# Pairing output blocks of two experts in a graph and mixture-of-experts kernel

## The chip, the cores and the metric

The kernel runs on one core of one Trainium2 chip. A core has TensorE (matmuls), VectorE, ScalarE, GpSimd and SyncE (SP), each with its own queue of instructions, and DMA engines that move data between HBM and the core. The metric is the device time of one execution in microseconds. Of the kernel before there are three runs: 798.14, 800.93 and 804.83 us, median 800.93 us.

## What is computed

The reference is one layer of a graph network, followed by a mixture of experts, on 625 nodes of 512 numbers. In short:

```python
x = x + relu(h_self + agg)          # h_self = LN(x) @ W_self.T + b_self
# agg: for each of 5000 edges, H_all[rel, tail] is added at its head
#      and H_all[rel + 8, head] at its tail; H_all = 16 relations of LN(x)
h = LN(x)                           # (625, 512)
router_logits = h @ router_w.T      # 16 experts
top_vals, top_idx = jax.lax.top_k(router_logits, 2)
weights = softmax(top_vals)         # two experts for each token
for wg, wu, wd, ce in experts:      # ce: the expert's weight for a token, or 0
    hid = silu(h @ wg) * (h @ wu)   # 512 -> 1024
    y = hid @ wd                    # 1024 -> 512
    acc = acc + ce[:, None] * y
out = x + acc
```

All is in float32. An expert's three matrices are 2 MB each. The kernel computes an expert only for the tokens that chose it.

## The kernel before

**First part.** For each of the 16 relations TensorE makes a table of transformed rows (L226), which goes to HBM as h_tab. GpSimd gathers the rows of the edges, 128 at a time (L466), in the order of a list made at L455. A one-hot matmul adds each gathered set into its tile of 128 nodes (L501, L508, L509). There are five tiles, 0 to 4, the last with fewer nodes. The messages of a tile come in stages; `add(j, s)` takes those of stage `s` for tile `j`, and `early_of` and `late` at L455 are the lists of the last two stages. When a tile has all its messages, its generator `rest(j)` does the routing: logits, the two best experts, and the place of each token among its expert's tokens (`place`). A hand-written list of steps sets how these generators and the messages alternate.

**Units.** The tokens of an expert are cut into units of 32. For one unit GpSimd fetches the tokens' rows (L682 for the first units, `fetch` at L848 for the others, up to eight units ahead), VectorE turns them (`turned`, L702), TensorE computes gate and up (`gate_up`, L714: 16 matmuls, four tiles of 32 columns at each of four steps of k), and ScalarE and VectorE make silu(gate) * up and turn it into hidT (`gated`, L726 to L732). A float32 matmul appears as two records in the trace. The PSUM tiles `o` of units are four.

**Output blocks.** `down` multiplies the hidden values of one expert's units with the expert's down matrix wd, over 8 steps of k. With more than two units it does one matmul per k of n * 32 columns on all 512 outputs (L745). With two units it does two matmuls per k, each of 64 columns on 256 outputs, which lie in the two halves of the partitions (L751). ScalarE copies the block out of PSUM (L757, or L759 with a weight), and GpSimd adds it into out in HBM by token (L760). Each such scatter waits for the one before it.

**Which experts and in what order.** Experts 0 to 2 (`NS = 3`) have three units each (`SU = 3`) before the ranking of the experts by load is known; the first two units of each (`SA = 2`) are told before tile 4 is routed, by `told_first` and `get_first`. These nine units are named o00 to o22, by expert and unit. Then come 13 ranks, in this order:

```python
RANKS = (3, 6, 3, 1)
ORDER = [12, 9, 10, 0, 11, 3, 4, 5, 6, 7, 8, 1, 2]
```

Ranks 0 to 2 have two units, 3 to 8 three, 9 to 11 four, and rank 12 (`r5`) five, as a block of three and one of two. The output block of one group of units is issued behind the units of the next (`waiting`, L1093 on). The words rank and expert are both used for these below.

**Tables.** `table` (L1026) multiplies one-hot matrices with what is to be told to each unit: `_t` (tokens, into `pw`), `_0` (weights of the first nine units, into `pv0`), and `_w` (weights of all other units, into `pw_w`). Their right sides val_t, val and val_w are made by VectorE at L1019. In the order on TensorE `_0` and a part of `_w` stand before the last five of the nine units, the rest of `_w` after them.

**Weights.** `load_expert` (L166) issues three loads on SP, gate, up and down (L176), into one of three pools that are used in turn. A load waits until the last matmul that reads the old contents of its buffer is done, and what stands behind it on SP waits too. The order of instructions on an engine is that of the program, except where the scheduler moves them by its own estimates; `tc.issue_after` holds some of them behind a named instruction.

## Time and profile before

| what | from | value |
|---|---|---|
| median of three runs | times | 800.93 us |
| the profiled execution | times | 802.45 us |
| its span, first to last instruction | page | 800.5 us |
| TensorE busy | page | 728.1 us, 91% |
| VectorE busy | page | 421.2 us, 53% |
| ScalarE busy | page | 133.1 us, 17% |
| GpSimd busy | page | 260.2 us, 32% |
| mean granted TensorE clock | cores | 0.950 |
| first unit starts | timeline of TensorE | 499.12 us |
| nine first units end | timeline of TensorE | 541.05 us |
| last output block ends | timeline of TensorE | 789.9 us |

The page gives busy time and the idle time before groups of instructions, with what ended it. The timeline lists the work of an engine in order: start, length, engine, line, operation, and in brackets the idle time before it and what it waited for. The busy time by window gives, for each stretch, the engines' busy time and counts, the granted clock as a share of full speed, the busy share of the DMA engines and what they moved. Ends of matmuls are modelled, so a busy TensorE need not be at its peak; starts are measured.

### The profile page before, as it was taken

The numbers are of one execution on the slowest core, as the hardware profiler recorded it, in microseconds if no ns is written. First come the engines' busy times: TensorE is split into PE (matmuls) and PEld (weight loads), VectorE is DVE, ScalarE is ACT, GpSimd is POOL, SyncE is SP. The second block draws the span as 40 slices with busy tenths as digits, with TensorE's granted clock in tenths as the row PEclk, the third lists the DMA queues.
The fourth block names the chain that finished last, engine by engine and source line by source line (L and its number), as shares of the span: only waits on it lengthen the run. The fifth ranks groups of instructions, "written<-read, shape, count | busy, mean of one in ns | idle before, by whom it ended". The sixth has DMA issues, their size and how long they took to land. (4 is left out here: it accounts for less than half of the span.)

```text
span 800.5 us, 9617 instructions
## 1 busy us (share of the span) xinstructions
PE 728.1 (91%) x3305; PEld 323.1 (40%) x3305; DVE 421.2 (53%) x1096; ACT 133.1 (17%) x252; POOL 260.2 (32%) x253
## 2 busy tenths in 40 slices
PE   5999998899968999959969986899999999999994
PEld 2444443355534555424535544223333333333332
DVE  7299937689758997426745837633223122222110
ACT  2000002223113332213322302000101001110010
POOL 1000017660275640575375352206333132200011
PEclk9999998999997999988988977889999999999998
DMA  6376449674487872786676397828999899999951
GB/s 205 127 261 236 178 139 298 210 246 151 140 266 231 261 234 74 234 280 188 217 221 188 126 365 287 296 87 301 387 382 366 312 390 395 383 394 389 381 189 15
DMA packets 77063, 200.70 MB, mean 251 GB/s; under 512 B 7636, under 2 KB 8072, under 8 KB 77008
## 3 DMA queue, kind: packets, MB, share of 16 engines
q1 hardware_dynamic: 46400, 125.57, 42.5%
q0 software_dynamic: 17936, 52.03, 22.7%
q10 hardware_dynamic: 12672, 22.42, 7.4%
q8 instruction: 28, 0.46, 0.2%
q14 instruction: 27, 0.22, 0.1%
HBM read 173.83 MB, written 26.87 MB: 251 GB/s over the span
## 5 line engine op out<-in xcount | busy, mean ns | idle before, releaser
L226 PE MATMUL o<-wt,xT 128*128 128x512 f32 x680 | 317.5, 611 | 2.7 <-ACT xT L217 2.7
L466 POOL DMA_INDIRECT g<-h_tab,rows x176 | 182.8, 1039 | 286.8 <-issue 151.3
L226 PEld LDWEIGHTS o<-wt,xT 128*128 128x128 f32 x680 | 131.7, 197 | 138.6 <-issue 130.6
L714 PE MATMUL o<-wgu,xbT 128*32 128x512 f32 x1600 | 179.0, 604 | 1.3 <-DVE in_unit L642 1.3
L505 ACT CAST hi<-g 128x512 fp32r<-128x512 f32 x158 | 91.3, 617 | 253.9 <-PE m L508 98.1
L507 DVE TENSOR_TENSOR lo<-g,hi 128x512 fp32r<-128x512 f32 x158 | 104.6, 688 | 40.5 <-ACT hi L505 23.8
L702 DVE STREAM_TRANSPOSE xbT<-xb 128x128 f32<-128x128 f32 x50 | 15.4, 310 | 165.8 <-PE o L714 156.6
L714 PEld LDWEIGHTS o<-wgu,xbT 128*32 128x32 f32 x1600 | 51.5, 112 | 123.9 <-issue 122.6
L508 PE MATMUL m<-hi,to 128*128 128x512 f32 x158 | 81.5, 516 | 20.4 <-issue 10.1
L745 PE MATMUL y<-wd,hidT 128*96 128x512 f32 (+1 forms) x208 | 91.9, 596 | 0.0
L295 DVE TENSOR_TENSOR hs<-o,bt 128x512 f32<-128x512 f32 x80 | 54.9, 688 | 60.6 <-PE o L226 33.4
L509 PE MATMUL m<-lo,to 128*128 128x512 f32 x158 | 70.5, 446 | 15.2 <-issue 6.8
L848 POOL DMA_INDIRECT xb<-hn_rows,get x41 | 39.2, 955 | 78.6 <-DVE xbT L702 49.7
L760 POOL DMA_INDIRECT out<-ys,adds x14 | 21.5, 1533 | 116.9 <-ACT ys L757 113.9
L745 PEld LDWEIGHTS y<-wd,hidT 128*96 128x96 f32 (+1 forms) x208 | 34.3, 169 | 56.7 <-issue 56.7
L508 PEld LDWEIGHTS m<-hi,to 128*128 128x128 f32 x158 | 30.6, 194 | 40.2 <-issue 21.7
L509 PEld LDWEIGHTS m<-lo,to 128*128 128x128 f32 x158 | 30.8, 195 | 38.5 <-issue 17.2
L726 ACT ACTIVATE sil<-o 128x256 f32<-128x256 f32 x50 | 19.2, 383 | 159.4 <-PE o L714 153.1
L416 DVE TENSOR_TENSOR val<-oc,vals 128x528 f16<-128x528 f16 x56 | 38.0, 709 | 0.0
L731 DVE SCALAR_TENSOR_TENSOR hid<-sil,weight,o 128x256 f32<-128x256 f32 x41 | 19.7, 481 | 30.1 <-ACT sil L726 26.4
L491 DVE TENSOR_TENSOR to<-count_f,node 128x512 fp32r<-128x512 f32 (+4 forms) x50 | 30.8, 623 | 6.1 <-issue 5.0
L401 DVE TENSOR_TENSOR at<-count_h,slot_p 128x768 f16<-128x768 f16 x28 | 26.7, 952 | 5.0 <-remote 5.0
(223 smaller groups left out, 354.2 us busy)
## 6 DMA issues: line engine op xcount, KB each, us to landing
wgu<-in_gate_w SPq DMA_DIRECT2D x16, 2048.0 KB
wgu<-in_up_w SPq DMA_DIRECT2D x16, 2048.0 KB
wd<-in_down_w SPq DMA_DIRECT2D x16, 2048.0 KB
h_tab<-hs ACTq DMA_DIRECT2D x80, 256.0 KB
wt<-in_w_rel SPq DMA_DIRECT2D x16, 1024.0 KB
bt<-in_b_rel SPq DMA_DIRECT2D x16, 256.0 KB
g<-h_tab,rows POOLq DMA_INDIRECT x176
xs<-in_x SPq DMA_DIRECT2D x5, 256.0 KB
```

What stands on the lines that cost most here:

```text
L226: nc.tensor.matmul(o, xT[:, k, ts(j, P)], wt[:, k, :], start=(k == 0), stop=(k == KD - 1))
L295: nc.vector.tensor_tensor(hs, linear(wt, j), bt, ALU.add)
L416: nc.vector.tensor_tensor(val[:, :, i, :], oc, vals[:, cs, i : i + 1].to_broadcast([P, SG, NCH]), ALU.mult)
L466: nc.gpsimd.indirect_dma_start(out=g, out_offset=None, in_=h_tab[d][: n * NP, :], in_offset=bass.IndirectOffsetOnAxis(ap=found[d][0][:, c ...
L491: nc.vector.tensor_tensor(to[:, :n], count_f[:, None, :].to_broadcast([P, n, P]), found[d][1][:, c : c + n, None].to_broadcast([P, n, P]), ...
L505: nc.scalar.copy(hi, g)
L507: nc.vector.tensor_tensor(lo, g, hi, ALU.subtract)
L508: nc.tensor.matmul(m, at, hi, start=first, stop=False)
L509: nc.tensor.matmul(m, at, lo, start=False, stop=last)
L714: last = nc.tensor.matmul(o[ts(c, Q), :].rearrange("p (s m i) -> p s m i", s=2, i=Q), xbT[:, k, :], wgu[:, k].rearrange("p s (m c i) -> p ...
L745: nc.tensor.matmul(y[: n * Q, :], hidT[:, k, :], wd[:, k, :], start=(k == 0), stop=(k == KF - 1))
L848: nc.gpsimd.indirect_dma_start(out=xb, out_offset=None, in_=hn_quarters, in_offset=bass.IndirectOffsetOnAxis(ap=get, axis=0),)
```

## The change

Four things change together.

1. `down` is divided. `add_outputs` takes pieces of one or two experts. Three units of one expert and one unit of another make one block of 128 rows: per k one matmul of 64 columns and two of 32, all on 512 outputs, of which the first two read one expert's wd and the third the other's. The two units that stay over from the second expert make a block in halves. The pairs are e0 with e1, e2 with the first unit of r5, and ranks 3 with 4, 5 with 6 and 7 with 8; the other four units of r5 make a block of their own. A block of two experts is added to out by two scatters, one after the other: the first takes the first 96 rows, the second all 128 with places that lie outside for rows not its own (`other_slots`, `AWAY`).
2. `load_expert` is divided into `load_hidden` (gate and up) and `load_output` (down). In the loop over ranks the gate and up of the next rank are issued before the down matrix of this one.
3. Softmax is issued earlier, and the tables of weights later: `_0` is held behind the eighth unit's last matmul and `_w` behind the ninth's. On TensorE both now follow the nine units, together with `_t`.
4. All of tile 3's last messages are gathered before the last two stages of tile 4, and the list of steps is changed to match.

```diff
--- before.py
+++ after.py
@@ -163,18 +163,32 @@
     n_again = const.tile([1, 1], I32, name="n_again")
     early = []
-    def load_expert(e):
+    def load_hidden(e):
         pool = wts[0]
         wts.append(wts.pop(0))
-        wgu = pool.tile([P, KD, 2, F], F32, name="wgu")
-        wd = pool.tile([P, KF, D], F32, name="wd")
-        for t, w in ((wgu[:, :, 0, :], gate_w), (wgu[:, :, 1, :], up_w), (wd, down_w)):
+        def load(t, w):
             s = w[e] if isinstance(e, int) else w[ds(e, 1)].rearrange("o k f -> (o k) f")
             behind = tc.issue_after(early.pop(0)) if early else nullcontext()
             with behind:
                 nc.sync.dma_start(t, s.rearrange("(k p) f -> p k f", p=P))
-        return wgu, wd
+        wgu = pool.tile([P, KD, 2, F], F32, name="wgu")
+        load(wgu[:, :, 0, :], gate_w)
+        load(wgu[:, :, 1, :], up_w)
+        def load_output():
+            wd = pool.tile([P, KF, D], F32, name="wd")
+            load(wd, down_w)
+            return wd
+        return wgu, load_output
+    def load_expert(e):
+        wgu, load_output = load_hidden(e)
+        return wgu, load_output()
     agg = act.tile([P, NT * D], F32, name="agg")
@@ -452,7 +466,7 @@
         early_of, late = ([cell[1, STAGES[1][g], j] for j in range(NT)] for g in (2, 3))
         relations_of = {(d, c): n for d, n, c0, cap, _ in plan for c in range(c0, c0 + cap)}
         order = [dc for _, cs in own_cells for dc in cs]
-        for cs in early_of[:4] + [late[0], late[1], early_of[4], late[2], late[3], late[4]]:
+        for cs in early_of[:4] + late[:4] + [early_of[4], late[4]]:
             order += cs
         order = [(d, relations_of[d, c], c) for d, c in order]
         assert len(set(order)) == 2 * NCH
@@ -735,33 +749,49 @@
             t = work.tile([P, KF, P], F32, name="hidT", bufs=3)
             return t if n == NQ else t.rearrange("p k t -> p (k t)")[:, : KF * n * Q].rearrange("p (k t) -> p k t", k=KF)
-        def down(wd, hidT, n, add, weight=None):
+        def down(y, pieces, wide):
+            for k in range(KF):
+                c = 0
+                for wd, hidT, g, n in pieces:
+                    if not wide:
+                        tiles = ((g, n, 0, slice(0, D // 2)), (g, n, 2, slice(D // 2, D)))
+                    elif n == 3:
+                        tiles = ((g, 2, c, slice(0, D)), (g + 2, 1, c + 2, slice(0, D)))
+                    else:
+                        tiles = ((g, n, c, slice(0, D)),)
+                    for u, m, at, cols in tiles:
+                        nc.tensor.matmul(
+                            y[at * Q : (at + m) * Q, : cols.stop - cols.start],
+                            hidT[:, k, u * Q : (u + m) * Q], wd[:, k, cols],
+                            start=(k == 0), stop=(k == KF - 1),
+                        )
+                    c += n
+        def add_outputs(pieces, add, weight=None):
+            wide = sum(n for *_, n in pieces) == 4
             y = py.tile([P, D], F32, name="y")
             ys = work.tile([P, D], F32, name="ys")
-            if n > 2:
-                for k in range(KF):
-                    nc.tensor.matmul(y[: n * Q, :], hidT[:, k, :], wd[:, k, :], start=(k == 0), stop=(k == KF - 1))
-                rows, width, to = n * Q, D, out
+            down(y, pieces, wide)
+            width, to = D, out
+            if not wide:
+                width, to = D // 2, out.rearrange("n (h d) -> (n h) d", h=2)
+            if weight is None:
+                nc.scalar.copy(ys[:, :width], y[:, :width])
             else:
-                for k in range(KF):
-                    for h in range(2):
-                        nc.tensor.matmul(
-                            y[ts(h, HP), : D // 2], hidT[:, k, :], wd[:, k, ts(h, D // 2)],
-                            start=(k == 0), stop=(k == KF - 1),
-                        )
-                rows, width, to = P, D // 2, out.rearrange("n (h d) -> (n h) d", h=2)
-            if weight is None:
-                nc.scalar.copy(ys[:rows, :width], y[:rows, :width])
-            else:
-                nc.scalar.mul(ys[:rows, :width], y[:rows, :width], weight[:rows])
-            nc.gpsimd.indirect_dma_start(
-                out=to, in_=ys[:rows, :width], in_offset=None,
-                out_offset=bass.IndirectOffsetOnAxis(ap=add[:rows], axis=0),
-                bounds_check=NP * D // width - 1, oob_is_err=False, compute_op=ALU.add,
-            )
+                nc.scalar.mul(ys[:, :width], y[:, :width], weight)
+            for i in range(len(pieces)):
+                rows = P if i == len(pieces) - 1 else pieces[0][3] * Q
+                nc.gpsimd.indirect_dma_start(
+                    out=to, in_=ys[:rows, :width], in_offset=None,
+                    out_offset=bass.IndirectOffsetOnAxis(ap=add[:rows, i : i + 1], axis=0),
+                    bounds_check=NP * D // width - 1, oob_is_err=False, compute_op=ALU.add,
+                )
         hn_quarters = hn_rows.rearrange("n (q d) -> (n q) d", q=NQ)
         xb0 = ract.tile([P, SU, NS, P], F32, name="xb0")
@@ -789,7 +819,7 @@
         early.extend(3 * stored)
         weights = [weights0, load_expert(1)]
-        for step in ((1, 3), 0, (4, 3), 0, (2, 3), 1, 0, 1, 0, 2, 1, (3, 3), 2, 1, 2, 3, 2, (4, 2), 3, 3, 3):
+        for step in ((1, 3), 0, 0, (2, 3), 1, 0, 1, 0, (3, 3), 2, 1, 2, 1, (4, 3), 3, 2, 3, 2, (4, 2), 3, 3):
             if isinstance(step, int):
                 next(tiles[step])
             else:
@@ -859,6 +889,11 @@
             nc.vector.tensor_tensor(row, row, token, ALU.add)
             nc.vector.tensor_scalar(row, row, -1.0, None, op0=ALU.add)
             return row
+        def other_slots(add, row):
+            nc.vector.tensor_scalar(add, row, 0.0, AWAY, op0=ALU.mult, op1=ALU.add)
+            nc.vector.tensor_copy(add[ts(NQ - 1, Q)], row[ts(NQ - 1, Q)])
         def by_slot(add, row, step, n):
@@ -993,14 +1028,13 @@
         last_units = []
         def last_unit():
-            for e in range(1, NS):
-                last_units.append(begun(e, 2))
-                last = steps(range(KD), last_units[-1])
-            last_units.append(last)
+            last_units.extend(begun(e, 2) for e in range(1, NS))
+            last_units.extend([steps(range(KD), o) for o in last_units])
         side, ends = units_of(place, cap, start, last_unit)
-        o12, o22, last = last_units
+        o12, o22, last_but, last = last_units
         gated(o21[0], None, hidT0[2], 1)
+        softmax()
         def of_units(unit, n, name):
             mine = mact.tile([P, 2 * NT, n], BF16, name=f"mine{name}")
@@ -1048,59 +1082,75 @@
         nc.vector.tensor_copy(who, pw)
         token, get_i = rows_to_get(who, "")
-        softmax()
         gated(o02[0], None, hidT0[0], 2)
         gated(o12[0], None, hidT0[1], 2)
         last_hid = gated(o22[0], None, hidT0[2], 2)
         pv0 = pr.tile([P, SU * NS, 3], F32, name="pv0", tag="pT")
-        table(mine0.rearrange("p c g s -> p c (g s)"), told[:, :, :, 2:], pv0, "_0")
+        with tc.issue_after(last_but):
+            table(mine0.rearrange("p c g s -> p c (g s)"), told[:, :, :, 2:], pv0, "_0")
         who0 = mact.tile([P, SU * NS, 3], F32, name="who0")
         nc.vector.tensor_copy(who0, pv0)
         nc.vector.tensor_scalar(token0, pw0, 1.0 / NQ, None, op0=ALU.mult)
         weight0 = summed(who0, "_0").rearrange("p (g s) -> p g s", s=NS)
         row0 = rows_to_add(token0.rearrange("p g s -> p (g s)"), "_0").rearrange("p (g s) -> p g s", s=NS)
-        add0 = mact.tile([P, NS], I32, name="add0")
+        halves0 = mact.tile([P, 2], F32, name="halves0")
+        nc.vector.tensor_scalar(halves0, row0[:, 1:, 1], 2.0, half, op0=ALU.mult, op1=ALU.add)
+        add0 = mact.tile([P, NS, 2], I32, name="add0")
         by0 = mact.tile([P, NS], F32, name="by0")
+        nc.vector.memset(by0, 1.0)
         for g in range(SU):
-            nc.vector.tensor_copy(add0[ts(g, Q), :], row0[ts(g, Q), g, :])
-            nc.vector.tensor_copy(by0[ts(g, Q), :], weight0[ts(g, Q), g, :])
+            nc.vector.tensor_copy(add0[ts(g, Q), ::2, 0], row0[ts(g, Q), g, ::2])
+            nc.vector.tensor_copy(by0[ts(g, Q), ::2], weight0[ts(g, Q), g, ::2])
+        other_slots(add0[:, 0, 1:], row0[:, 0, 1:2])
+        nc.vector.tensor_copy(by0[ts(3, Q), 0:1], weight0[ts(3, Q), 0, 1:2])
+        for q in range(NQ):
+            nc.vector.tensor_copy(add0[ts(q, Q), 1, 0:1], halves0[ts(q, Q), q % 2 : q % 2 + 1])
+            nc.vector.tensor_copy(by0[ts(q, Q), 1:2], weight0[ts(q, Q), 1 + q % 2, 1:2])
         pw_w = pr.tile([P, NU, 3], F32, name="pw_w", tag="pT")
-        table(mine, told[:, :, :, 2:], pw_w, "_w")
+        with tc.issue_after(last):
+            table(mine, told[:, :, :, 2:], pw_w, "_w")
         who_w = mact.tile([P, NU, 3], F32, name="who_w")
         nc.vector.tensor_copy(who_w, pw_w)
         weight = summed(who_w, "")
-        for e in range(NS):
-            down(weights[e][1], hidT0[e], SU, add0[:, e : e + 1], by0[:, e : e + 1])
+        wd0 = [w[1] for w in weights]
+        add_outputs([(wd0[0], hidT0[0], 0, 3), (wd0[1], hidT0[1], 0, 1)], add0[:, 0], by0[:, 0:1])
+        add_outputs([(wd0[1], hidT0[1], 1, 2)], add0[:, 1], by0[:, 1:2])
         to_row = rows_to_add(token, "")
...
-        blocks = []
-        for r in ORDER:
+        other_slots(add0[:, 2, 1:], to_row[:, C5 : C5 + 1])
+        adds4 = mact.tile([P, RANKS[2]], I32, name="adds4")
+        by_slot(adds4, to_row[:, C4:C3], 4, 4)
+        adds5 = mact.tile([P, 1], I32, name="adds5")
+        by_slot(adds5, to_row[:, C5 + 1 : C2], 4, 4)
+        adds3 = mact.tile([P, RANKS[1] // 2, 2], I32, name="adds3")
+        by_slot(adds3[:, :, 0], to_row[:, C3:C5], 6, 3)
+        other_slots(adds3[:, :, 1], to_row[:, C3:C5].rearrange("p (i s) -> p i s", s=6)[:, :, 3])
+        pairs3 = to_row[:, C3:C5].rearrange("p (i s) -> p i s", s=6)[:, :, 4:]
+        pairs2 = to_row[:, C2:].rearrange("p (i s) -> p i s", s=2)
+        halved = {}
+        for n, pairs in ((3, pairs3), (2, pairs2)):
+            nc.vector.tensor_scalar(pairs, pairs, 2.0, half, op0=ALU.mult, op1=ALU.add)
+            halved[n] = mact.tile([P, pairs.shape[1]], I32, name=f"halved{n}")
+            for q in range(NQ):
+                nc.vector.tensor_copy(halved[n][ts(q, Q), :], pairs[ts(q, Q), :, q % 2])
...
+        load_next()
+        waiting = []
+        for i, r in enumerate(ORDER):
+            if i > 0:
+                load_next()
+            wgu, load_output = loaded[i]
+            wd = load_output()
+            if i == 0:
+                load_next()
+            us = columns_of(r)
+            hid = [hidden(1), hidden(4)] if r == r5 else [hidden(len(us))]
+            for g, u in enumerate(us):
                 with tc.issue_after(last_hid):
                     xbT = turned(rows.pop(0))
                 o, _ = gate_up(wgu, xbT)
-                gated(o, weight[:, c + g : c + g + 1], hidT, g)
+                at_g = (hid[0], 0) if r == r5 and g == 0 else (hid[-1], g - (r == r5))
+                gated(o, weight[:, u : u + 1], *at_g)
                 fetch_next()
-            if waiting is not None:
-                down(*waiting)
-            i = (c - first[n]) // n
-            waiting = (wd, hidT, n, adds[n][:, i : i + 1])
-        down(*waiting)
+            for job in waiting:
+                add_outputs(*job)
+            waiting = []
+            if r == r5:
+                add_outputs([(wd0[2], hidT0[2], 0, 3), (wd, hid[0], 0, 1)], add0[:, 2], by0[:, 2:3])
+                waiting.append(([(wd, hid[1], 0, 4)], adds5))
+            elif r >= r4:
+                waiting.append(([(wd, hid[0], 0, 4)], adds4[:, r - r4 : r - r4 + 1]))
+            elif r >= r3:
+                k = (r - r3) // 2
+                if (r - r3) % 2 == 0:
+                    kept = wd, hid[0]
+                else:
+                    add_outputs([(*kept, 0, 3), (wd, hid[0], 0, 1)], adds3[:, k])
+                    add_outputs([(wd, hid[0], 1, 2)], halved[3][:, k : k + 1])
+            else:
+                waiting.append(([(wd, hid[0], 0, 2)], halved[2][:, r : r + 1]))
+        for job in waiting:
+            add_outputs(*job)
         n_more = mact.tile([1, 1], I32, name="n_more")
...
+                add_outputs([(wd, hidT, 0, NQ)], add)
```

More of the change, by code (lines that the diff above doesn't have):

```diff
@@ L1074 @@
         weight = summed(who_w, "")
-        for e in range(NS):
-            down(weights[e][1], hidT0[e], SU, add0[:, e : e + 1], by0[:, e : e + 1])
+        wd0 = [w[1] for w in weights]
+        add_outputs([(wd0[0], hidT0[0], 0, 3), (wd0[1], hidT0[1], 0, 1)], add0[:, 0], by0[:, 0:1])
+        add_outputs([(wd0[1], hidT0[1], 1, 2)], add0[:, 1], by0[:, 1:2])
         to_row = rows_to_add(token, "")
-        nc.vector.tensor_scalar(to_row[:, C5 + 3 :], to_row[:, C5 + 3 :], 2.0, half, op0=ALU.mult, op1=ALU.add)
@@ L1081 @@
-        adds = {}
-        for n, c, e in ((4, C4, C3), (3, C3, C5 + 3), (2, C5 + 3, NU)):
-            adds[n] = mact.tile([P, (e - c) // n], I32, name=f"adds{n}")
-            by_slot(adds[n], to_row[:, c:e], n, n)
-        for g in range(2):
-            nc.vector.tensor_copy(
-                adds[2][ts(2 + g, Q), :],
-                to_row[ts(2 + g, Q), C5 + 3 : NU].rearrange("p (i s) -> p i s", s=2)[:, :, g],
-            )
-        blocks = []
-        for r in ORDER:
-            if r == r5:
-                blocks += [(r, C5, 3), (r, C5 + 3, 2)]
-            elif r >= r4:
-                blocks.append((r, C4 + 4 * (r - r4), 4))
-            elif r >= r3:
-                blocks.append((r, C3 + 3 * (r - r3), 3))
-            else:
-                blocks.append((r, C2 + 2 * r, 2))
@@ L1102 @@
-        ahead = 8
-        columns = [u for _, c, n in blocks for u in range(c, c + n)]
+        other_slots(add0[:, 2, 1:], to_row[:, C5 : C5 + 1])
[6 more added lines that the diff above has]
+        other_slots(adds3[:, :, 1], to_row[:, C3:C5].rearrange("p (i s) -> p i s", s=6)[:, :, 3])
@@ L1104, with columns_of @@
+        def columns_of(r):
+            if r == r5:
+                return range(C5, C2)
+            if r >= r4:
+                return range(C4 + 4 * (r - r4), C4 + 4 * (r - r4) + 4)
+            if r >= r3:
+                return range(C3 + 3 * (r - r3), C3 + 3 * (r - r3) + 3)
+            return range(C2 + 2 * r, C2 + 2 * r + 2)
+        columns = [u for r in ORDER for u in columns_of(r)]
         rows = []
@@ L1109, in fetch_next, with load_next @@
                 rows.append(fetch(get_i[:, u : u + 1]))
-        for _ in range(ahead):
+        for _ in range(8):
             fetch_next()
-        first = {4: C4, 3: C3, 2: C5 + 3}
-        held = waiting = None
-        for r, c, n in blocks:
-            if r != held:
+        loaded = []
+        def load_next():
+            if len(loaded) < len(ORDER):
+                r = ORDER[len(loaded)]
                 e = nc.values_load(
@@ L1120 @@
                 )
-                wgu, wd = load_expert(e)
-                held = r
-            hidT = hidden(n)
-            for g in range(n):
+                loaded.append(load_hidden(e))
+        load_next()
[10 more added lines that the diff above has]
+            for g, u in enumerate(us):
                 with tc.issue_after(last_hid):
@@ L1242 @@
                     gated(o, weight[:, g : g + 1], hidT, g)
-                down(wd, hidT, NQ, add)
+                add_outputs([(wd, hidT, 0, NQ)], add)
 def kernel(x, src, dst, edge_type_8, L0_gnn_W_self, L0_gnn_b_self, L0_gnn_W_rel, L0_gnn_b_rel,
```

## The prediction

> **What bounds the kernel now.** I read the page's forty slices first (TensorE 9 tenths busy nearly everywhere after 640 us), then busy time by window from 498 us to the end.
>
> ```profile
> 498.00:505.00 7.00, 5.88 (x32) 1.48 (x36) 2.70 (x15) 0.68 (x1) 2.82 (x3) 0.52 0.99 332
> ...
> 514.00:522.00 8.00, 2.41 (x31) 0.73 (x24) 7.73 (x29) 0.38 (x1) 3.44 (x3) 0.77 0.40 131
> 522.00:526.00 4.00, 4.00 (x27) 1.33 (x30) 1.57 (x9) 0.00 (x0) 0.00 (x0) 0.61 0.02 6
> 526.00:534.00 8.00, 8.00 (x80) 2.44 (x76) 2.04 (x5) 0.77 (x2) 0.00 (x0) 1.00 0.00 0
> ...
> 640.00:700.00 60.00, 60.00 (x460) 19.99 (x452) 14.49 (x36) 6.22 (x16) 17.34 (x16) 1.00 1.04 389
> 700.00:760.00 60.00, 60.00 (x373) 19.26 (x366) 12.74 (x31) 5.58 (x13) 4.86 (x4) 1.00 1.03 388
> 760.00:771.00 11.00, 11.00 (x75) 3.33 (x74) 1.85 (x4) 1.35 (x3) 1.43 (x1) 1.00 0.96 334
> 771.00:790.00 19.00, 18.91 (x140) 8.06 (x138) 1.85 (x4) 1.72 (x4) 2.99 (x2) 1.00 0.14 22
> 790.00:800.50 10.50, 0.00 (x0) 0.00 (x0) 0.00 (x0) 0.37 (x1) 1.56 (x1) 0.73 0.14 19
> ```
>
> The columns are window and its length, busy time of TensorE, its weight loads, VectorE, ScalarE and GpSimd, then granted clock, DMA share and GB/s. From 522 us TensorE never rests until 789.9 us; the DMA is as full from 562 to 771 us, but its last 19 us are empty. So TensorE sets the end, with the weights 15 us behind it. The last 10.6 us are the copy and scatter of the last block. The timeline of TensorE gives the price of each block, and the place of the one hole:
>
> ```profile
> 499.12 11.51 PE L714 MATMUL o<-wgu,xbT 128*32 128x512 f32 x80 [1.26 <-DVE in_unit L642]
> ...
> 522.00 0.47 PE L1026 MATMUL pw_w<-val_w,at 128*128 128x123 bf16 x3 [5.59 <-DVE val_w L1019]
> 522.43 18.69 PE L714 MATMUL o<-wgu,xbT 128*32 128x512 f32 x160
> ```
> ```profile
> 579.87 7.11 PE L745 MATMUL y<-wd,hidT 128*96 128x512 f32 x16
> 586.91 13.94 PE L714 MATMUL o<-wgu,xbT 128*32 128x512 f32 x128
> 600.78 3.67 PE L751 MATMUL y<-wd,hidT 128*64 128x256 f32 x32
> 604.38 13.94 PE L714 MATMUL o<-wgu,xbT 128*32 128x512 f32 x128
> 618.25 7.13 PE L745 MATMUL y<-wd,hidT 128*128 128x512 f32 x16
> ...
> 782.78 7.13 PE L751 MATMUL y<-wd,hidT 128*64 128x256 f32 x64
> ```
>
> A unit (16 matmuls, two records each) is 13.94 / 4 = 3.48 us. An output block costs 7.05 us from start to start (579.87 to 586.91) whether it has 96 or 128 columns; a block in halves 3.60 (600.78 to 604.38). A three-unit block pays for a column group that it leaves empty.
>
> **The change, part by part.**
>
> Output blocks. Before, 13 full blocks (e0, e1, e2, three units of r5, three ranks of four units, six of three) and 4 in halves. After, 9 full (e0+e1, e2+r5, r5's other four, the three fours, three pairs of ranks) and 7 in halves (e1's two, two of each pair, ranks 0 to 2). If a mixed block costs what a full one does: 4 x 7.05 - 3 x 3.60 = 17.4 us less on TensorE. All of it is on the path, since TensorE has no hole there.
>
> Five of the nine are mixed: per step of k a tile of 64 columns, then two of 32. No row shows this. What the trace has is uniform: 32-column tiles start four at a time every 0.43 us, 64-column halves two every 0.215 us, a full tile one every 0.43 us. Columns times time is the same in all, which speaks for 0.86 us a step in the mixed block too. Against it stands the Trainium skill, "TensorEngine Tiling (Array Packing)", section Tiling Modes, under Key Properties: changing the mode, not just the tile, drains TensorE; its list has 128x64 and 128x32 as modes, none of both. The mixed block changes twice a step, 16 times a block, 80 times in all. The nearest rows are the changes at block edges: the last L714 record starts at 600.256 and the first L751 at 600.777, 0.52 us where the pitch is 0.43; back, 604.074 to 604.382, 0.31 where it is 0.215. So a change costs 0.09 to 0.10 us, up to 0.17 with the slower step after it. By the rows' columns alone the five blocks add nothing; by the rule at the row's price they add 80 x 0.1 = 8 us (0 to 13.6). I take 8: net 9.4 less. A gain from switching is excluded, since no group runs faster than its columns.
>
> Scatters go from 17 to 20, as each mixed block writes twice, one after the other. One takes about 1.5 us on GpSimd (row of L760: 21.5 us in 14) and the next can start 2.7 us later. They queue ahead of fetches of xb, which run eight units (28 us) ahead: two scatters, 8.6 us, hide there. If that cover went, each would cost TensorE up to 4.3 us. At the end two half blocks now follow each other at 3.6 us, less than 4.3: the tail grows by 0.7, to 11.3 us. ScalarE copies 128 rows for 96 (585 against 581 ns): nothing.
>
> Weights' loads. Gate and up of the next expert are issued before this one's down matrix on SP. In the timeline of SP a down load waits for its buffer until TensorE ends the block (wd at 744.36, then gate at 745.24), with everything behind it on SP. With gate and up ahead the pairs can hold both down matrices without stopping the stream. The DMA needs 17.7 us per expert (twelve between 548.9 and 770.9 with about 4 idle, including fetches and scatters); a pair takes TensorE 2 x 10.5 + 8.65 + 3.6 = 33.2 us against 35.4 of DMA, so there the weights are the pacer, and eat into the 15 us by which they lead. I count zero, and check the floor below.
>
> Early stage. Tile 3's three late gathers move ahead of tile 4's three first ones (1.256 us each on GpSimd, about 3.8 us), and its messages before tile 4's. The first fetch needs tiles 0 to 3, waits 20.6 us for its list and starts at 494.2; so o00 may start 3.8 us sooner, 495.3. The tables of weights, L1026, are told after the ninth unit instead of between units; the 5.59 us hole goes, and with it the slow steps behind it (granted clock 0.61 from 522 to 526: 1.6 us). What is late next: TensorE comes to o02 after o20 and o21 (7 us), at 512 + 7 = 519 us, where its xb was transposed at 519.99 in the trace; and o22 waits for the PSUM buffer that o20's hid frees, which stands behind val_w (1.40 us) on VectorE. These overlap in part: I charge 1.5 us (0 if VectorE is early, 4 if it keeps its times and both add up with the told tables). The steps at half clock at the start stay. Saved: 3.8 + 5.6 + 1.6 - 1.5 = 9.5; for e2's weights (issued 496.4, gate and up landing no sooner than 507) I round down to 8 (4 to 9). Fourteen more small copies on VectorE, about 0.16 to 0.22 us each, lie beside output blocks where it is 5.5 of 7.9 us busy: nothing; without that cover 2.8 us.
>
> Floor by DMA: r5's gate and up come with e0's last unit, its down with the first block, both 8 to 9 us sooner. The stream that ended at 770.9 ends near 762; after it only the last half block is needed, 3.6 us: 766. TensorE ends at 789.9 - 9.4 - 8 = 772.5, later, so it still decides.
>
> Sum: 772.5 + 11.3 = 783.8 us of span, against 800.5. The profiled execution was 802.45 us, 1.95 over its span: 785.8. It stood 1.5 above the median of the runs, so 784.
>
> **Rivals.**
>
> 1. Switches are free. TensorE would end at 764, and the DMA floor decides: 766 + 11.3 = 777 span, 777 or 778 us. For it: the equal price per column. Against: every mode change in the trace costs 0.09 us or more. Chance 0.12.
>
> 2. The early gain doesn't come: VectorE's chain of tables, 7.7 of 8 us busy from 514 to 522, ends no sooner, and the wait moves to the ninth unit or the first output block. Then 800.5 - 9.4 + 0.7 = 791.8 of span, 792 us; the loads start no sooner either, and their end at 767 (771 less the idle 4) leaves that standing. For it: that VectorE row. Against: 17.6 us of its work lie in the 29 us from 505 to 534. Chance 0.17.
>
> 3. Slower: tiles of two widths don't overlap at all. Each step is then the 64 tile's two passes (0.86 us), the two passes of both 32 tiles together (0.86), and two changes (0.2): 1.92 us, so 15.4 us a mixed block. Five times 8.35 more is 41.8, in place of the 8: TensorE ends 789.9 - 17.4 + 41.8 - 8 = 806.3, and the time is 818 us. It decides from 12 us a mixed block, 0.31 us a change, where it has eaten the other gains (17.4 + 8 - 0.7 = 24.7, over five blocks 4.9). For it: the rule, and that no row shows tiles of two widths side by side. Against: the measured price of a change is a third of that point. Chance 0.22.
>
> 4. The change doesn't do what it says: the scheduler sets units of the next expert between the 64 tiles and the 32 tiles of two of the pairs, so part of the alternation is gone (fewer changes), but a 64 tile alone would leave half the columns empty, 3.4 us a block. Two blocks: +7 less 3 of changes, about 788. It falls in my own case's range.
>
> **How the numbers follow.** My case with the fourth rival has 0.46 (range 779 to 790), and 0.03 stay for mishaps that make it slower. A measurement tells this kernel from no change at about 1%, 8 us. Under 793 lie my case, the first and most of the second; between 793 and 809 the rest of it and the milder end of the third; above it the third and the mishaps: 0.63, 0.13, 0.24. The range goes from the first rival's end, 775, to just short of the third's value, 816.
>
> **What would show it.** In the changed profile: mixed blocks of 8 to 9 us between units (7.05 would be rival 1, over 12 rival 3); no hole before 541 and the ninth unit ending near 533; first unit near 495; last weights landing at 757 to 764; TensorE busy through to about 772; a tail of 11 us. The prediction is wrong if the mixed steps are longer than 1.1 us, if TensorE stands before an output block for a down matrix, or if units wait for xb behind scatters.

## The result, and the profile after

The changed kernel takes 828.12 us (median of four runs, 825.37 to 831.49) against 799.53 us (four runs) for the kernel before: a ratio of 1.036, with a 95% interval of 1.027 to 1.044. It is slower, where 784 us was forecast, and outside the range of 775 to 816. The profiled execution, the longest of the four, took 831.49 us, with a span of 829.5.

The timeline of TensorE in the changed kernel, from the first unit on (start, length, engine, line, operation; in brackets the idle time before it and what it waited for):

```profile
499.24 8.97 PE L728 MATMUL o<-wgu,xbT 128*32 128x512 f32 x64 [0.69 <-issue]
...
515.07 0.19 PE L687 MATMUL pw<-tok,at 128*128 128x3 f16 x2 [3.07 <-DVE tok L682]
515.19 21.66 PE L728 MATMUL o<-wgu,xbT 128*32 128x512 f32 x198
536.78 0.56 PE L1060 MATMUL pw<-val_t,at 128*128 128x82 bf16 x10
...
538.08 19.14 PE L765 MATMUL y<-wd,hidT 128*64 128x512 f32 x73
557.55 0.38 PE L765 MATMUL y<-wd,hidT 128*64 128x256 f32 x1 [0.33 <-issue]
...
560.27 17.37 PE L728 MATMUL o<-wgu,xbT 128*32 128x512 f32 x160
...
684.23 10.51 PE L728 MATMUL o<-wgu,xbT 128*32 128x512 f32 x96
694.67 19.55 PE L765 MATMUL y<-wd,hidT 128*64 128x512 f32 x80
714.15 20.81 PE L728 MATMUL o<-wgu,xbT 128*32 128x512 f32 x192
```

The stretch at 694.67 is the mixed block of ranks 3 and 4 and the half block (a block in halves) behind it, 19.48 us to the next unit. The windows of both (columns as in the prediction) and of what follows:

```profile
694.67:710.55 15.88, 15.88 (x53) 2.68 (x49) 1.24 (x3) 0.38 (x1) 0.96 (x1) 1.00 1.01 391
710.55:714.15 3.60, 3.60 (x34) 2.20 (x32) 0.00 (x0) 0.59 (x1) 1.49 (x1) 1.00 0.66 170
```
```profile
640.00:700.00 60.00, 60.00 (x424) 19.67 (x418) 13.89 (x34) 5.77 (x14) 15.98 (x15) 1.00 1.04 384
700.00:760.00 60.00, 60.00 (x392) 16.67 (x392) 8.66 (x21) 4.61 (x11) 8.13 (x6) 1.00 0.86 314
760.00:815.60 55.60, 55.60 (x414) 17.90 (x406) 9.90 (x23) 4.79 (x12) 7.71 (x5) 1.00 0.53 173
815.60:829.50 13.90, 0.03 (x2) 0.00 (x0) 0.00 (x0) 0.37 (x1) 3.12 (x2) 0.68 0.16 20
```

A half block costs the same 3.60 us as before. A mixed block costs 15.88 us, where a full one costs 7.05. TensorE reads busy throughout and the DMA, full before, is now at 0.86 and 0.53 of its time: the weights wait for TensorE. "Busy" hides the loss, because a matmul that fills half the columns counts as much as one that fills all.

The starts of the matmul records in one step of that block show what happens (us; each float32 matmul leaves two records, which are called its passes here):

```
694.667  64 columns, first pass
695.147  64 columns, second pass           +0.480
695.670  32 columns, 32 columns            +0.523
696.123  32 columns, 32 columns            +0.453
696.652  64 columns, next step of k        +0.529
```

One pass after another, 1.985 us a step. The two passes of the 64-column tile do not run side by side, and no 32-column tile runs beside it.

The difference of the two profiled spans, 29.0 us, by stretch:

| stretch | before | after | difference |
|---|---|---|---|
| start to last gather of messages | 472.6 | 475.7 | +3.1 |
| last gather to first output block | 69.2 | 62.3 | -6.9 |
| first output block to end of TensorE | 248.1 | 277.5 | +29.4 |
| end of TensorE to end of span | 10.6 | 13.9 | +3.3 |

The first row can't be read as an effect of the change: between single executions on one chip below it differs by up to 17 us (462.7 to 479.3), also where the kernels hardly differ there. That is why the early stage is read from the last gather on.

### The profile page after: what moved, and what is told of

Read it like the earlier page. It is cut to its first block, busy times and chain, and to the rows that moved or that the text cites. A ratio compares the mean times of both kernels' runs of the same rounds, so it can differ in the third digit from the quotient of the medians.

```text
span 829.5 us, 10046 instructions
## 1 busy us (share of the span) xinstructions
PE 751.9 (91%) x3497; PEld 318.5 (38%) x3497; DVE 425.0 (51%) x1122; ACT 131.8 (16%) x251; POOL 264.9 (32%) x257
## 5 line engine op out<-in xcount | busy, mean ns | idle before, releaser
L480 POOL DMA_INDIRECT g<-h_tab,rows x176 | 180.5, 1026 | 292.2 <-issue 153.9
L765 PE MATMUL y<-wd,hidT 128*64 128x256 f32 (+3 forms) x528 | 136.9, 511 | 1.3 <-issue 1.3
L522 PE MATMUL m<-hi,to 128*128 128x512 f32 x158 | 82.0, 519 | 21.0 <-ACT hi L519 15.4
L523 PE MATMUL m<-lo,to 128*128 128x512 f32 x158 | 70.7, 448 | 17.4 <-DVE agg L529 7.9
L765 PEld LDWEIGHTS y<-wd,hidT 128*64 128x64 f32 (+2 forms) x528 | 41.3, 134 | 96.8 <-issue 86.5
L790 POOL DMA_INDIRECT out<-ys,adds x10 | 15.7, 1566 | 115.8 <-ACT ys L785 95.0
L740 ACT ACTIVATE sil<-o 128x256 f32<-128x256 f32 x50 | 19.2, 384 | 155.9 <-PE o L728 148.8
L430 DVE TENSOR_TENSOR val<-oc,vals 128x528 f16<-128x528 f16 x56 | 37.8, 705 | 0.0
```

The lines of the kernel that those rows point to most:

```text
L430: nc.vector.tensor_tensor(val[:, :, i, :], oc, vals[:, cs, i : i + 1].to_broadcast([P, SG, NCH]), ALU.mult)
L480: nc.gpsimd.indirect_dma_start(out=g, out_offset=None, in_=h_tab[d][: n * NP, :], in_offset=bass.IndirectOffsetOnAxis(ap=found[d][0][:, c ...
L522: nc.tensor.matmul(m, at, hi, start=first, stop=False)
L523: nc.tensor.matmul(m, at, lo, start=False, stop=last)
L765: nc.tensor.matmul(y[at * Q : (at + m) * Q, : cols.stop - cols.start], hidT[:, k, u * Q : (u + m) * Q], wd[:, k, cols], start=(k == 0), st ...
```

## Experiments

The theory after the result (A): a tile runs beside others only if they have the same width; a 64-column tile among 32-column ones has no partner, so half the array idles for both its passes, and again for the 32-column pair; each change of width costs a little more. The rivals: the block is slow because it reads two experts' matrices or issues three matmuls a step (B); the changes of width are all of the loss (C); a 64-column tile on 512 outputs is slow by itself (K). For the three other parts of the change, and for a pause in the first half block, the rivals are named with their runs. Each group of runs stands beside the kernel before on the same chip, whose median was 800.1 us for the first four, 803.99 for the next four, 760.88 for three and 805.25 for the last, so ratios are compared and not times.

**Uniform tiles.**

```diff
-                        tiles = ((g, 2, c, slice(0, D)), (g + 2, 1, c + 2, slice(0, D)))
+                        tiles = tuple((g + i, 1, c + i, slice(0, D)) for i in range(3))
```

> Mixed blocks made of four tiles of 32 columns in place of one of 64 and two of 32; all else as in the changed kernel. Theory A (a 64-column tile among 32-column ones runs alone, one pass after the other, and each change of width costs 0.13 us): the step of k falls from 1.985 to 0.86 us, a mixed block from 15.9 to 7.05, five blocks give back 44 us, and the time is 782 to 788 us, faster than the kernel before. Rival B (the mixed block is slow since it reads two experts' hidden values and two down matrices, or since three matmuls a step are issued): the block stays at 14 to 16 us and the time at 828.

Measured: 789.35 us, ratio 0.986 (0.981 to 0.991). One edit of one line turns 3.6% slower into 1.4% faster. The block of the second pair of ranks, in the timeline of this run, together with its half block:

```profile
685.92 10.65 PE L765 MATMUL y<-wd,hidT 128*32 128x512 f32 x96
696.51 20.81 PE L728 MATMUL o<-wgu,xbT 128*32 128x512 f32 x192
```

10.59 us for both, so 6.99 for the mixed block. It reads the same two experts and issues more matmuls, so B falls. The time missed the expectation by 1 to 7 us; the pause in the first half block, which had grown by 8.7 us (below), is enough to explain it.

**The same tiles, the widths apart.** All eight steps of the 64-column tile first, then all eight of the 32-column tiles: 2 changes of width a block for 16.

```diff
-            for k in range(KF):
-                c = 0
-                for wd, hidT, g, n in pieces:
...
+            groups = [all_tiles[:1], all_tiles[1:]] if len(all_tiles) == 3 else [all_tiles]
+            for group in groups:
+                for k in range(KF):
```

> Mixed blocks with the same tiles (one of 64 columns, two of 32), but all eight steps of the 64-column tile first and then all eight of the two others: 2 changes of width a block in place of 16. Theory A (occupancy counts most): the two stretches take 8 x 0.86 us each, 13.9 us a block, so five blocks give back 10 us of the changes alone, 818 us. Rival C (the changes are all of it, and within one width a tile's two passes run side by side): 7.3 us a block, 785 us.

Measured: 814.27 us, ratio 1.020 (1.013 to 1.027).

```profile
687.65 17.68 PE L769 MATMUL y<-wd,hidT 128*64 128x512 f32 x80
705.26 20.81 PE L728 MATMUL o<-wgu,xbT 128*32 128x512 f32 x192
```

17.61 us with the half block, 14.01 for the mixed one. So of the 8.8 us that a mixed block costs too much, 1.87 went with 14 of the 16 changes of width, 0.134 us each, and 6.9 to 7.0 stay with the lone tiles and the two changes that are left. C falls. The two 32-column tiles on their own start as a pair every 0.42 to 0.43 us, at the pace of four.

**Two tiles of 64 columns.** Run with uniform tiles and fewer fetches (below). It leaves out the first expert's third unit and the second expert's unit in the mixed blocks, and computes the first's units 1 and 2 in their place, again with its own down matrix.

```diff
-                for wd, hidT, g, n in pieces:
+                for wd, hidT, g, n in pieces[:1]:
...
-                        tiles = tuple((g + i, 1, c + i, slice(0, D)) for i in range(3))
+                        tiles = ((g, 2, c, slice(0, D)), (g + 1, 2, c + 2, slice(0, D)))
```

> As the run with uniform tiles and fewer fetches, but a mixed block is two tiles of 64 columns: the second takes units 1 and 2 of the first expert again, with its down matrix. Left out: the first expert's third unit and the second expert's unit in these blocks. Theory A (what costs is two widths in one block, and a tile with no partner of its own width): 0.86 us a step, 7.05 us a block, within 3 us of the uniform run, 782 to 788 us. Rival K (a 64-column tile on all 512 outputs is slow by itself): 1.3 us a step or more, 800 us or more.

Measured: 734.88 us beside 760.88, ratio 0.966 (0.961 to 0.970); the run with four tiles that is otherwise the same had 0.974 (0.967 to 0.982) on another chip.

```profile
517.71 7.09 PE L765 MATMUL y<-wd,hidT 128*64 128x512 f32 x32
524.73 3.64 PE L728 MATMUL o<-wgu,xbT 128*32 128x512 f32 x32
```

7.02 us for the block of e2 and r5: K falls, two equal tiles of 64 columns start together and take what four of 32 do. The expected time in us was written for a chip of the usual speed; this one was 5% faster for the kernel before.

**The pause in the first half block, and the fetches.** In the changed kernel the first mixed block and its half block take 22.19 us (538.08 to 560.27) against 19.48 for the second pair. In the run with uniform tiles it is 22.0 against 10.6, and the half block falls apart:

```profile
547.57 0.42 PE L765 MATMUL y<-wd,hidT 128*64 128x256 f32 x1 [0.78 <-issue]
548.27 0.38 PE L765 MATMUL y<-wd,hidT 128*64 128x256 f32 x1 [0.29 <-issue]
...
551.83 4.12 PE L765 MATMUL y<-wd,hidT 128*64 128x256 f32 x6 [1.00 <-issue]
...
558.89 0.59 PE L765 MATMUL y<-wd,hidT 128*64 128x256 f32 x1 [0.73 <-issue]
559.41 18.62 PE L728 MATMUL o<-wgu,xbT 128*32 128x512 f32 x160
```

TensorE waits for nothing that the profile shows; it gets a matmul every 0.7 us or less often. ScalarE's copy of the first block stands too, in the same run, and so does SP (its loads come 1.4 us apart at 556 to 559):

```profile
558.20 0.69 ACT L787 ACTIVATE ys<-y,by 128x512 f32<-128x512 f32 x1 [21.58 <-remote]
```

Meanwhile GpSimd issues fourteen fetches one behind the other, 539.05 to 556.6. The earlier in such a run the half block begins, the longer the pause: 14.3 us after its first fetch in the changed kernel (2.7 us of pause), 12.4 in the run with the widths apart (5.6), 5.4 here (11.4). Eight are the lead, the others follow as buffers come free. The edit makes them six:

```diff
-                xbT = work.tile([P, KD, Q], F32, name="xbT", bufs=4)
+                xbT = work.tile([P, KD, Q], F32, name="xbT", bufs=2)
-            xb = work.tile([P, P], F32, name="xb", bufs=10)
+            xb = work.tile([P, P], F32, name="xb", bufs=4)
-        for _ in range(8):
+        for _ in range(3):
             fetch_next()
```

> Mixed blocks of four 32-column tiles, and fewer fetches in a row: fetches run 3 units ahead in place of 8 (xb in 4 buffers for 10, xbT in 2 for 4), so that GpSimd issues 6 and not 14 one after the other at the first output blocks. Theory F (while GpSimd issues fetches back to back the other engines get their instructions slowly, and TensorE lives on what it holds): the half block of e1, which took 15 us for 3.6, loses at most 2 us, and the time falls from 789 to 778 to 782 us. Rival G (TensorE waits there for something else, or only where a trace is taken): no change, 788 to 791 us. If the fetches come too late for their units, 795 us or more, with waits for xb in the trace.

Measured: 784.75 us, ratio 0.974 (0.967 to 0.982), where the run without the edit had 0.986. Here is the first pair in its timeline, and the same copy on ScalarE:

```profile
540.28 10.68 PE L765 MATMUL y<-wd,hidT 128*32 128x512 f32 x96
550.88 17.37 PE L728 MATMUL o<-wgu,xbT 128*32 128x512 f32 x160
```
```profile
547.95 0.69 ACT L787 ACTIVATE ys<-y,by 128x512 f32<-128x512 f32 x1 [8.46 <-PE y L765]
```

10.60 us: the pause is gone, and with it the late copy. The six fetches come as four and, 2.3 us later, two. The time is 3 to 7 us above what was expected; on TensorE the gain is 11.9 us (243.4 to 231.5 from the first block to its end), in the medians some 9. The edit also brought a wait of its own: with two buffers for xbT, TensorE stands 1.54 us before o02 for a turned xb.

The same edit on the changed kernel alone:

> The changed kernel with fewer fetches in a row (3 units ahead, xb in 4 buffers, xbT in 2) and nothing else. Theory F (the half block of e1 loses 2.7 us there while GpSimd issues fourteen fetches): 2 to 3 us less, 824 to 826 us, and no pause in that block. Rival G (the pause comes from elsewhere): 828 us and the pause stays.

Measured: 783.21 beside 760.88 us, ratio 1.028 (1.024 to 1.032) where the changed kernel has 1.036, on a chip that is faster than the expectation assumed. In its timeline the first pair takes 19.48 us (492.18 to 511.66), as the second does, and the 2.7 us are gone:

```profile
492.18 19.55 PE L765 MATMUL y<-wd,hidT 128*64 128x512 f32 x80
511.66 17.38 PE L728 MATMUL o<-wgu,xbT 128*32 128x512 f32 x160
```

That a long run of fetches makes the pause is shown; the smaller number of xbT buffers is not what removes it, since the last run below has four again and no pause. That the engines' instructions are what comes late is only inferred, from the fact that three engines stand at once without a visible wait. The transfers don't settle it: in the run with uniform tiles, from 547.2 to 558.9 us, the DMA engines move 72 GB/s in the mean, so they are not full, and no packet of instructions is among what they move. The kernel before has thirteen fetches in a row at this place and no pause; its full blocks of 96 columns need four instructions (two loads of weights, two matmul records) in 0.86 us, half blocks and 32-column tiles sixteen. That this is the reason is not tested.

**The other parts of the change.** Output blocks as before, everything else changed (against the kernel before; the list of steps and the tables as in the change):

```diff
-        for cs in early_of[:4] + [late[0], late[1], early_of[4], late[2], late[3], late[4]]:
+        for cs in early_of[:4] + late[:4] + [early_of[4], late[4]]:
...
-                wgu, wd = load_expert(e)
+                if i > 0:
+                    load_next()
+                wgu, load_output = loaded[i]
+                wd = load_output()
+                if i == 0:
+                    load_next()
```

> The output blocks of the kernel before, with the three other parts of the change (loads of gate and up ahead of down, weights' tables last, tile 3's messages first). Theory A: the first nine units end 4 us sooner as in the changed kernel, the loads give nothing, 795 to 797 us. Rival D (the other parts cost time themselves, by waits that the mixed blocks cover): 800 us or more.

Measured: 793.71 us, ratio 0.988 (0.984 to 0.992). So the other parts gain 1.2%, a little more than expected; all of the slowdown and more is in the blocks. Then without the loads' order, and with the tables alone, whose edit (softmax earlier with it) is

```diff
-        table(mine0.rearrange("p c g s -> p c (g s)"), told[:, :, :, 2:], pv0, "_0")
+        with tc.issue_after(last_but):
+            table(mine0.rearrange("p c g s -> p c (g s)"), told[:, :, :, 2:], pv0, "_0")
...
-        table(mine, told[:, :, :, 2:], pw_w, "_w")
+        with tc.issue_after(last):
+            table(mine, told[:, :, :, 2:], pw_w, "_w")
```

> The kernel before with the tables last and tile 3's messages first, loads and blocks as before. Theory A (loads in another order give nothing as long as each block needs one down matrix): as with all three parts, 792 to 795 us. Rival H (the order of loads is part of the gain): 797 us or more.

> The kernel before with the weights' tables told last, and nothing else. Theory T (the hole of 5.6 us and the slow clock behind it are what is gained early): 793 to 795 us. Rival O (tile 3's messages first are needed as well, or are the gain): 797 us or more.

Measured: 796.61 us, ratio 0.990 (0.983 to 0.997), and 793.29 us, ratio 0.989 (0.983 to 0.995). The first time, on a chip where the kernel before took 804 us, lies between its two expectations and decides nothing; the second is what theory T expected. The three ratios cannot be told apart. The traces can, though each is of one execution. From the last gather to the first unit, and from there to the first output block:

| kernel | to first unit | to first block | sum |
|---|---|---|---|
| before | 26.5 | 42.7 | 69.2 |
| tables last alone | 25.6 | 35.0 | 60.6 |
| tables and messages' order | 23.8 | 37.8 | 61.6 |
| these and the loads | 23.4 | 37.8 | 61.3 |

The tables give 8.6 us. The messages' order brings the first unit 1.8 us sooner and loses 2.9 behind it, at a wait that is new:

```profile
510.00 3.62 PE L714 MATMUL o<-wgu,xbT 128*32 128x512 f32 x26
515.91 0.19 PE L673 MATMUL pw<-tok,at 128*128 128x3 f16 x2 [2.30 <-DVE tok L668]
```

TensorE stands for tile 4's places, which VectorE makes late. The loads' order changes nothing in these stretches.

The early parts undone, with uniform tiles (the tables' edit above and the two lists, turned back):

```diff
-        for cs in early_of[:4] + late[:4] + [early_of[4], late[4]]:
+        for cs in early_of[:4] + [late[0], late[1], early_of[4], late[2], late[3], late[4]]:
...
-        with tc.issue_after(last):
-            table(mine, told[:, :, :, 2:], pw_w, "_w")
+        table(mine, told[:, :, :, 2:], pw_w, "_w")
```

> Mixed blocks of four 32-column tiles as in the run before, but the tables' places and the order of messages and steps of the kernel before. Theory A: 4 us more than with them, 786 to 792 us. Rival E (the weights' stream is now the pacer, so an earlier start of the units is worth nothing, or the later start costs the loads as much again): within 1 us of the run with them, or 8 us and more above it.

Measured: 802.08 us, ratio 1.001 (0.998 to 1.004), some 12 us above the run with them (0.986): rival E's number. But its cause is not shown: of the traces' stretches 8.6 us are early (70.2 against 61.6 from last gather to first block) and 1.6 lie in the blocks, where the pause is there again. That the weights' stream costs anything I could not find.

The loads together again, with uniform tiles:

```diff
             wd = load_output()
-            if i == 0:
-                load_next()
```

> Mixed blocks of four 32-column tiles, with gate, up and down of each expert issued together as in the kernel before. Theory A (with pairs a down load waits until the pair's block, and holds gate and up of the next expert behind it on SP): TensorE waits for gate and up in the pairs, 5 to 15 us more than with the loads divided, 794 to 804 us. Rival Z (the lead of the weights covers it): within 2 us of it, 788 to 791 us.

Measured: 795.78 us beside 803.99, ratio 0.988 (0.986 to 0.991); with the loads divided 0.986 (0.981 to 0.991). No difference by ratio, and theory A's wait did not come: in the trace there is no wait for gate and up in the pairs; TensorE stands 1.54 and 1.55 us before the last two half blocks, which now follow their own units directly, and the pause costs 13.4 us for 11.4. What the divided loads are worth stays open within that.

**A better version.** Uniform tiles, fewer fetches, loads divided, tables last, and the messages' order of before (the run with fewer fetches, with the two lists turned back):

```diff
-        for cs in early_of[:4] + late[:4] + [early_of[4], late[4]]:
+        for cs in early_of[:4] + [late[0], late[1], early_of[4], late[2], late[3], late[4]]:
```

> Uniform tiles, fewer fetches, loads divided and tables last, with the order of messages and steps of the kernel before. Theory T (the messages' order gives 2.5 us on the first unit and loses 2.8 us behind it, at the wait for tile 4's places): within 2 us of the run with it, 782 to 787 us, and no wait of TensorE between the first and the ninth unit. Rival O (the order is part of the gain): 788 us or more.

Measured: 741.93 beside 760.88 us, ratio 0.973 (0.969 to 0.976). As good as with the messages' order, but with a pause of 3.33 us before the fifth unit, which was not expected. With four buffers for xbT again, and xb in three:

```diff
-                xbT = work.tile([P, KD, Q], F32, name="xbT", bufs=2)
+                xbT = work.tile([P, KD, Q], F32, name="xbT", bufs=4)
-            xb = work.tile([P, P], F32, name="xb", bufs=4)
+            xb = work.tile([P, P], F32, name="xb", bufs=3)
-        for _ in range(3):
+        for _ in range(2):
```

> As the run named best, but xbT keeps its four buffers (two there made the fifth unit wait for its turned rows, 3.3 us of TensorE) and xb has three, with fetches two units ahead: seven fetches in a row at the first output blocks. Theory X (the two xbT buffers are the cause of that pause): no wait of TensorE between the first and the ninth unit, 3 us less than best against the kernel before, a ratio of 0.966 to 0.971. Rival Y (the pause has another cause, or seven fetches starve the half block again): a ratio of 0.973 or more, with the pause or with slow steps in the half block of e1.

Measured: 782.58 beside 805.25 us, ratio 0.971 (0.965 to 0.978). The pause is gone:

```profile
501.56 10.28 PE L728 MATMUL o<-wgu,xbT 128*32 128x512 f32 x80 [1.26 <-DVE in_unit L656]
511.77 0.20 PE L687 MATMUL pw<-tok,at 128*128 128x3 f16 x2
511.91 22.52 PE L728 MATMUL o<-wgu,xbT 128*32 128x512 f32 x208
534.37 0.56 PE L1060 MATMUL pw<-val_t,at 128*128 128x82 bf16 x10
```

From first unit to first block it takes 34.1 us for 39.6, so the xbT buffers were the cause of the pause (X; the fetches whose buffers changed too come only after this stretch). The half block of e1 has no pause either: the seven fetches come as three, three and one, and the first pair takes 10.6 us. But the ratio lies between the two expectations and its interval covers both. In this execution the first unit came 31.7 us after the last gather, for 25.9 before; I have no cause for that. By their ratios both versions beat the kernel before by nearly 3%, and the changed one by 6%.

## Why the prediction was wrong

**The step that failed is the price of a mixed block.** The prediction put it at 7.05 us plus 16 changes of 0.1, 8.65 in all, from "columns times time is the same in all". It is 15.88. That rule holds for tiles of one width side by side, and I took it for a property of the array. The four records that start together every 0.43 us are one pass each of four different tiles; when one tile has no partner, its passes follow each other and the columns beside it stay empty. The starts in the changed kernel show it, and the runs with the widths apart (14.01 us), with four tiles of 32 (6.99) and with two of 64 (7.02) leave none of the rivals B, C and K. Why tiles of two widths don't run side by side no run here shows. I had written that no row shows two widths side by side, and yet let the rows of one width decide. Of the signs of being wrong that the prediction named, the first came true: a step of 1.985 us, above 1.1.

**The third rival was the right one.** It put the step at 1.92 us and the block at 15.4; measured 1.985 and 15.88. It got 0.22, and the range ended at 816, just short of its 818. The Trainium skill's rule on changes of mode ("TensorEngine Tiling (Array Packing)", section Tiling Modes), which I weighed against the rows, was right in sign, and the price that I read for it from the block edges, 0.09 to 0.17 us, was near the 0.134 of the run with the widths apart. (The first edge was read a little low: from the last record of one group to the first of the next the usual distance there is 0.41 us and not 0.43, so it gives 0.11.) But all changes together are 1.9 to 2.1 us of the 8.8 that a block loses; the page's list of modes, which has none of two widths, was the part that should have decided.

**The other rivals.** The 15.88 us of a block rule out the first (switches are free), the 6.9 us gained early the second. What the fourth said of the scheduler is so, in the blocks of ranks 5 with 6 and of 7 with 8:

```profile
734.89 1.62 PE L765 MATMUL y<-wd,hidT 128*64 128x512 f32 x3
735.90 0.64 PE L728 MATMUL o<-wgu,xbT 128*32 128x512 f32 x3
```

But the 26 and 50 records of the next expert's units all stand in the first step of k, and the other seven steps alternate as before. Less the units' own 0.108 us a record, block and half block take about 19.3 and 19.2 us, for 19.48 without them. The fourth rival's lone 64-column tile was the right mechanism, charged to two blocks in place of five. At 735.9 one 32-column tile of the block starts together with three of the unit: a partner can come from another expert's matrices, if it has the same width.

**Blocks saved: right.** With uniform tiles and no pause, the stretch from the first block to TensorE's end falls from 248.1 to 231.5 us, 16.6 for the 17.4 worked out. So the pairing is worth what it was meant to be, if its tiles are of one width.

**The early stage: right in sum, partly by luck.** I forecast 8 us (4 to 9) and measured 6.9, with 8.6 from the tables alone. The first unit came 3.0 us sooner from the last gather for 3.8 forecast; the wait that took the hole's place is 3.07 us at tok and not 1.5 at val_w or o02.

**The tail: mis-sized.** Forecast 11.3 us, measured 13.9. GpSimd in the changed kernel, the scatters at the end:

```profile
797.18 1.44 POOL L790 DMA_INDIRECT out<-ys,adds  x1 [28.92 <-ACT ys L785]
806.56 1.56 POOL L790 DMA_INDIRECT out<-ys,adds  x1 [7.93 <-DMA out<-ys,adds]
811.05 1.56 POOL L790 DMA_INDIRECT out<-ys,halved  x1 [2.93 <-DMA out<-ys,adds]
815.63 1.56 POOL L790 DMA_INDIRECT out<-ys,halved  x1 [3.02 <-issue]
820.64 1.56 POOL L790 DMA_INDIRECT out<-ys,halved  x1 [3.44 <-DMA out<-ys,halved]
```

The five scatters from the last mixed block on form one chain: the first, of 96 rows on all 512 outputs, is 9.4 us before the next, while those behind it follow each other in 4.5 to 5.0. I had taken 4.3 for all and counted only the last two. In the run with the widths apart that first scatter is issued 14.8 us before the last two half blocks begin, in place of 11.3, and the tail is 10.5.

**Floors and loads: right that the weights would not set the end.** In the changed kernel they wait for TensorE. With uniform tiles and fewer fetches the DMA is at 1.04 of its time from 551 to 760 us, and the last down load is issued at 752.4, so it is close.

**Not foreseen:** the pause of 2.7 us in the first half block (11 in the run with uniform tiles). The prediction hid fetches behind their lead of eight units and did not ask what the lead itself does to the others.

By the stretches: -6.9 early, -17.4 for blocks saved, +44.2 for five mixed blocks (5 x 8.83, the price of the one block taken for all), +2.7 for the pause, +3.3 for the tail, +3.1 before the gathers' end; 29.0 us.

## What to carry to other kernels

Put tiles of one width side by side: if a block is to be filled by 96 and 32 columns, make it of four 32s, not of one 64 and two 32s: beside two of 32 the 64-column tile ran alone, one pass after the other, and a row of busy time did not show it. A price taken from uniform rows does not hold for a mixture that no row shows; give the case in which they don't overlap the larger chance, or measure one block first. When blocks get faster, look at what is issued in a long run beside them, here GpSimd's lead of fetches.

## What the hardware showed that I had not expected

Beside blocks that need sixteen instructions in 0.86 us, a run of fourteen indirect fetches on GpSimd, issued every 1.26 us, slows TensorE, ScalarE and SP together: with uniform tiles the half block of 3.6 us took some 15, a matmul coming every 0.7 us or more, and with six fetches it took 3.6. Why is open. Two 32-column tiles on their own start a pair every 0.42 to 0.43 us, no faster than four. A change of tile width, at 512 outputs in float32, costs 0.134 us (1.87 us for 14).
